# Offset convolution of a deformable layer: six products for four output rows in place of four products for two

## The chip, the cores and the metric

The kernel runs on one core of a Trainium2 chip. The time is the device time of one execution in microseconds (us); three executions of the kernel before gave 1509.89, 1511.71 and 1513.13 us, median 1511.71. A core has four compute engines that matter here, each with its own queue of instructions that it takes strictly in order: TensorE (PE, matrix products; its weight loads are listed apart as PEld), VectorE (DVE), ScalarE (ACT) and GpSimd (POOL). SyncE (SP) mostly starts DMA transfers. Products land in PSUM, eight banks of 2 KB per partition (512 f32 numbers each); DVE or ACT has to read them out from there before the bank is free again.

## The reference

`x` has 8 images of 128 channels, 64x64 pixels, float32. Two layers are applied, each as `x + layer(groupnorm(x))`:

```python
om  = conv3x3(x, off_w) + off_b              # 128 -> 27 channels
off, mask = om[:, :18], sigmoid(om[:, 18:])  # two offsets and a mask for each of 9 taps
val = bilinear_sample(x, tap position + off) * mask
y   = einsum('bckhw,ock->bohw', val, w) + b  # deformable 3x3 convolution, 128 -> 128
layer0 = relu(batchnorm(y) * gamma + beta)
layer1 = mixture of 4 expert 3x3 convolutions (top 2, gated per image) + shared 3x3 convolution
```

The change is in the first line, the 3x3 convolution to the 27 offset and mask channels, and only for images 1 to 7.

## The kernel before

**Stages.** `dense()` does layer 0 for all images, `layer1()` does layer 1. `general()` is a fallback for large offsets; it is compiled, and does not run with these inputs. All instructions of `dense()` are in the order in which the program writes them (a manual schedule): every engine's queue is the order of emission.

**Bands.** `dense()` walks over 64 bands `g`, eight for each image (`NB = 8`), each of eight output rows. For a band, `sample` (L704) multiplies transposed pixels `xts` by weights `s` in five groups `q`; the products `pq` (three PSUM buffers, L714) are copied by ACT into `samples` (L724). `weights` (L683, DVE, L698) makes `s` three groups ahead (`AHEAD = 3`): at the start of band `g` DVE first makes groups 3 and 4 of that band, then, after `put_off()` (statistics of the last output and `close`, which copies the edges of `samples`, L740 to L747), groups 0 to 2 of the next band. Then `conv(g - 1)` (L751) does nine products `py` (L763) for the band before, 18 after the last band of an image, as that one has two output spans.

**What runs between the taps.** After each tap of `conv` the loop at L867 emits a little of other work, by the number of the tap, "part": at 0, 1, 5, 6 a quarter of the next band's pixels is transposed (`pixels`, L665: PE product `pt` into PSUM tag `pc`, then an ACT copy); at 1, 3, 5, 7 half of the x weights is prepared (`spread`, L642: ACT L648, then DVE L650); at 4 `pick` (L652) copies the pixels of a later band on DVE. And it calls `tick()` three times for a tap (four in image 0; three for two taps where there are 18).

**The generator `tables(b)`.** Each `tick()` advances `tables(b)` by one `yield`. It makes everything that image `b` needs ahead of its own bands: group norm (L309 to L337, ACT and DVE normalise four chunks each), the offset convolution (L340 to L416), a turned copy of the result (L422), stores to DRAM (SP, L427, L432), loads in another layout (`raw_off`, L465, L452), then distances, masks and the tables for x and y (L505 to L582). `pause(n)` spends `n` ticks. `yield BLOCK` makes the generator wait until the next tap among 2, 3, 4, 7; that is for PSUM: the tag `pc` has one buffer, shared by the pixels and by the products of the offset convolution. For image `b + 2` the generator is started in band 7 of image `b` and is drained ahead of band 6 of image `b + 1`; for image 1 the first part is done ahead of band 0, and the rest runs in bands 1 to 5 of image 0.

**The offset convolution before.** It is a minimal-filtering scheme in the row direction: two output rows from four products instead of six. For each `j` in 1, 2, 0, 3 `combine(j)` (L348) makes a difference or a sum of two sets of rows of the normalised image in `combos[0]` or `combos[1]` (two DVE instructions of 128x1024), and `block(j)` (L392) does one product: three taps `kx`, each as four matmuls of 512 columns (504 at the edge taps), with 32 output channels each and the four quarters of the image side by side in PSUM (`pc[32 * q : 32 * q + 32]`). The combined weights `offu_sb` are made once at the start (L802 to L806). ACT and DVE gather the four products into `om` (L402, L408, L409, L413, L415). The block of `j = 1` falls into the first band of the image before (part 7), those of 2, 0, 3 into the second band (parts 2, 4, 7), for images 3 to 7; for image 1 into bands 1 and 2 of image 0 (part 7, then 2, 4, 7), for image 2 into bands 0 and 1 of image 1 (parts 3, 7, then 2, 3).

Of the kernel before, what the change touches and what calls it, by code (L numbers as in the profile page):

```python
# [8 lines left out]
F32 = mybir.dt.float32  # L9
I32 = mybir.dt.int32  # L10
AF = mybir.ActivationFunctionType
ALU = mybir.AluOpType
# [4 lines left out]
P = 128  # L17
H = W = 64
# [4 lines left out]
CH = 512  # L23
# [6 lines left out]
NE = 4  # L30
# [21 lines left out]
ROWPAD = REACH  # L52
# [4 lines left out]
BLOCK = "block"  # L57
# [7 lines left out]
def deform_moe_conv(  # L65
# [18 lines left out]
    nc = tc.nc  # L84
# [3 lines left out]
    small = ctx.enter_context(tc.tile_pool(name="small", bufs=2))  # L88
# [6 lines left out]
        out=gsel, in_=gsel, compare_op=ALU.is_ge, fill=0.0, base=0,  # L95
# [3 lines left out]
        out=gsel, in_=gsel, compare_op=ALU.is_ge, fill=0.0, base=3,  # L99
# [78 lines left out]
    def dense():  # L178

        with ExitStack() as st:  # L180
            st.enter_context(tc.manual_schedule())
            a1 = st.enter_context(tc.tile_pool(name="d1", bufs=1))
# [3 lines left out]
            ps_c = st.enter_context(tc.tile_pool(name="ps_c", bufs=1, space=PSUM))  # L186
# [9 lines left out]
            offw_sb = a1.tile([P, TAPS, 32], F32, name="offw_sb")  # L196
            nc.gpsimd.memset(offw_sb[:, :, 27:32], 0.0)

            offu_sb = [a1.tile([P, 3, 32], F32, name=f"offu_sb{i}") for i in range(2)]
            offb_sb = a1.tile([P, 1], F32, name="offb_sb")  # L200
            nc.gpsimd.memset(offb_sb, 0.0)
            ident = a1.tile([P, P], F32, name="ident")
# [60 lines left out]
            def pause(n):  # L263
                for _ in range(n):
                    yield
# [34 lines left out]
            def tables(b):  # L300
# [3 lines left out]
                pad = pads[b % 2]  # L304
# [43 lines left out]
                def combine(j):  # L348

                    lo, hi, op = (  # L350
                        (0, 2, ALU.subtract), (1, 2, ALU.add), (2, 1, ALU.subtract),
                        (1, 3, ALU.subtract),
                    )[j]
                    for half in range(2):
                        rows = [
                            pad[:, ROWPAD - 1 + H // 2 * half + i :][:, 0 : H // 2 : 2]
                            for i in (lo, hi)
                        ]
                        n = H // 4
                        (nc.vector if b or j == 1 or half == 0 else nc.gpsimd).tensor_tensor(  # L360
                            combo_of[j][:, half * n : half * n + n], *rows, op
                        )
                        yield from pause(2)
# [25 lines left out]
                def taken(j):  # L389
                    return pcs.pop(j).rearrange("p (t w) -> p t w", w=W)  # L390

                def block(j):  # L392

                    yield BLOCK
                    for kx in (1, 0, 2):
                        tap(j, kx)
                    yield from pause(2)

                for j in (1, 2):
                    yield from combine(j)  # L400
                yield from block(1)
                nc.scalar.activation(even, taken(1), AF.Identity, bias=offb_sb)  # L402
                yield from combine(0)
                yield from block(2)
                if b == 0:
                    yield from combine(3)
                m2 = taken(2)
                nc.vector.tensor_tensor(odd, even, m2, ALU.subtract)  # L408
                nc.vector.tensor_tensor(even, even, m2, ALU.add)  # L409
                if b:  # L410
                    yield from combine(3)
                yield from block(0)
                nc.vector.tensor_tensor(even, even, taken(0), ALU.add)  # L413
                yield from block(3)
                nc.vector.tensor_tensor(odd, odd, taken(3), ALU.subtract)  # L415
                yield  # L416
                by_rows = omr.rearrange("p (h w) -> p h w", w=W)
                turned = omc.rearrange("p w h -> p h w")
                for half in (slice(0, H // 8), slice(H // 8, H // 4)):
# [46 lines left out]
                        by_column.append((k, outs, parts, v))  # L466
                for k, *where in by_column:
                    turned_in(nc.sync if b or k == 0 else nc.gpsimd, k, *where)
                yield from pause(50)

                def moved(side, t, *dims):

# [373 lines left out]
            for g in range(len(bands) + 1):  # L846
                b, j = bands[g] if g < len(bands) else (B, 0)
                if j == NB - 2:
                    for _ in made:
                        pass  # L850
                    asked, made, means_of = True, iter(()), statistics(b + 2)
                turned = pixels(g + 1) if g + 1 < len(bands) else iter(())
                for q in range(NGR):
                    if g < len(bands):
                        if g or q + AHEAD < NGR:
                            weights(g * NGR + q + AHEAD)
                        sample(g * NGR + q)
                        if q == 2:
                            load_x(g + 3, nc.gpsimd)
                        if q in (2, 3):  # L860
                            for k in range(T * (q - 2), T * (q - 1)):
                                load_y(g + 2, k, nc.gpsimd)
                    if q == 1:
                        put_off()
                taps = conv(g - 1) if g else iter(())
                twice = 2 if g and bands[g - 1][1] == NB - 1 else 1
                for done, _ in enumerate(taps):  # L867
                    part, odd = divmod(done, twice)
                    if odd == 0 and part in PIXELS:
# [12 lines left out]
                    for _ in range(3 + (g < NB) if twice == 1 else 1 + done % 2):  # L882
                        tick()
                    if odd == 0 and part == 4:
                        if g + 2 < len(bands):
                            pick(g + 2)
                        if 2 <= j < 6:
                            load_quarter(b + 2, j - 2)
                for _ in turned:
                    pass  # L890
                if g == 0:
                    pick(2)
                    for slots in HALVES:
# [238 lines left out]


    def layer1():
        yscale = small.tile([P, 1], F32, name="yscale")
        rsqrt(yscale, ymv[:, 1:2], BN_EPS)
        nc.vector.tensor_tensor(yscale, yscale, gamma_sb, ALU.mult)
        yshift = small.tile([P, 1], F32, name="yshift")
        nc.vector.tensor_tensor(yshift, ymv[:, 0:1], yscale, ALU.mult)
        nc.vector.tensor_tensor(yshift, beta_sb, yshift, ALU.subtract)  # L1140
        with ExitStack() as st:
# [58 lines left out]
            def prepare(b, made):  # L1200
# [79 lines left out]
                tot = small.tile([P, 1], F32, name="tot")  # L1280
# [3 lines left out]
                mb = small.tile([P, NE], F32, name="mb")  # L1284
# [186 lines left out]
```

## Time and profile before

| what | us |
|---|---|
| median of three runs | 1511.71 (1509.89 to 1513.13) |
| profiled execution | 1505.04, of which the span of the profile is 1502.9 |
| PE, DVE, ACT, POOL busy | 1361.4, 973.0, 826.5, 503.8 |
| idle time of PE between 200 and 1010 us of the span | 28 of 810 |
| a group of the offset convolution on PE (24 records) | 2.76 |
| one `combine` instruction, 128x1024 (L360) | 1.22 |
| one addition from PSUM into `om`, 128x512 (L408) | 0.69 |

All lines in fences are from the profile of one execution. Times are us from the start of its span. A line of the order of time has the start, the duration from the first start to the last end, the engine, the line of the kernel, the operation, output and inputs by the program's names, the shape, and the number of instructions; in square brackets stands how long the engine was idle before it and what ended that. A float32 matmul is two records of PE, so a block of 12 matmuls is "x24". The windows view gives, for each stretch, the busy time of the engines in the order PE, PEld, DVE, ACT, POOL with the number of instructions in parentheses, then the granted PE clock (1.00 is full speed), and the DMA share and rate.

### The profile page before, as it was taken

The numbers are of one execution on the slowest core, as the hardware profiler recorded it, in microseconds if no ns is written. First come the engines' busy times: TensorE is split into PE (matmuls) and PEld (weight loads), VectorE is DVE, ScalarE is ACT, GpSimd is POOL, SyncE is SP. The second block draws the span as 40 slices with busy tenths as digits, with TensorE's granted clock in tenths as the row PEclk, the third lists the DMA queues.
The fourth block names the chain that finished last, engine by engine and source line by source line (L and its number), as shares of the span: only waits on it lengthen the run. The fifth ranks groups of instructions, "written<-read, shape, count | busy, mean of one in ns | idle before, by whom it ended". The sixth has DMA issues, their size and how long they took to land.

```text
span 1502.9 us, 21333 instructions
## 1 busy us (share of the span) xinstructions
PE 1361.4 (91%) x7714; PEld 761.9 (51%) x7714; DVE 973.0 (65%) x1904; ACT 826.5 (55%) x1123; POOL 503.8 (34%) x775
## 2 busy tenths in 40 slices
PE   4279799999999998999999999999974899999998
PEld 1245465656556555555555565566642344444443
DVE  5555475576567647656765765645518888889872
ACT  2365674776587468658757865866724233322320
POOL 6333342433334233333423433344203222333200
PEclk9589899999999999999999999999996999999999
DMA  4485775986698497669748876788607134444111
GB/s 145 115 172 132 170 163 109 210 189 137 129 210 190 96 199 196 136 130 206 191 100 192 211 150 132 164 200 190 148 23 303 56 141 168 168 167 154 56 43 58
DMA packets 130940, 227.28 MB, mean 151 GB/s; under 512 B 82003, under 2 KB 88303, under 8 KB 122137
## 3 DMA queue, kind: packets, MB, share of 16 engines
q0 software_dynamic: 50928, 122.40, 38.7%
q1 hardware_dynamic: 78880, 102.93, 22.1%
q8 instruction: 63, 1.03, 0.3%
q10 hardware_dynamic: 1017, 0.50, 0.1%
q14 instruction: 52, 0.43, 0.1%
HBM read 180.23 MB, written 45.35 MB: 150 GB/s over the span
## 4 chain that ended last, share of the span: by engine, by line
PE 67%; DMA 11%; ACT 10%; DVE 5%; issue 3%; SPq 3%; POOL 1%; ACTq 0%; DVEq 0%; POOLq 0%
PE py L763 22%; PE pc L1383 21%; PE pq L714 12%; PE pt L672 5%; PE pc L379 5%; DMA ywts<-taby 3%; DMA xwts<-tabx 2%; ACT xwts L648 2%; ACT xt L677 2%; ACT work L537 1%; ACT samples L724 1%; DMA pad<-in_x_dram 1%; ACT work L541 1%; SPq L432 1%; DMA colwise<-om 1%
## 5 line engine op out<-in xcount | busy, mean ns | idle before, releaser
L763 PE MATMUL py<-samples,dw_sb 128*128 128x512 f32 (+3 forms) x1296 | 576.9, 562 | 7.1 <-ACT y L771 5.3
L617 POOL DMA_DIRECT2D ywts<-taby x504 | 303.3, 618 | 281.4 <-DMA xwts<-tabx 236.0
L714 PE MATMUL pq<-s,xt 64*128 64x144 f32 (+1 forms) x3840 | 284.3, 301 | 34.3 <-DVE s L698 21.8
L724 ACT COPY samples<-pq 128x864 f32<-128x864 f32 (+1 forms) x320 | 280.7, 973 | 36.0 <-PE pq L714 35.8
L714 PEld LDWEIGHTS pq<-s,xt 64*128 64x128 f32 x3840 | 257.9, 190 | 83.1 <-issue 23.5
L763 PEld LDWEIGHTS py<-samples,dw_sb 128*128 128x128 f32 x1296 | 217.0, 190 | 160.3 <-issue 133.5
L677 ACT COPY xt<-pt 128x512 f32<-128x512 f32 (+1 forms) x256 | 142.2, 555 | 206.7 <-PE pt L672 206.3
L698 DVE TENSOR_TENSOR s<-xwts,ywts 128x72 f32<-128x72 f32 (+1 forms) x447 | 199.3, 499 | 84.1 <-PE pq L714 42.0
L650 DVE TENSOR_SCALAR xwts<-xwts 128x1152 f32<-128x1152 f32 (+2 forms) x130 | 97.4, 749 | 185.9 <-ACT xwts L648 185.7
L672 PEld LDWEIGHTS pt<-ident,picked 128*128 128x128 f32 x960 | 111.1, 141 | 170.5 <-ACT xt L677 103.9
L632 POOL DMA_DIRECT2D xwts<-tabx x128 | 73.0, 574 | 349.1 <-DVE s L698 307.6
L1383 PE MATMUL pc<-v,u 128*128 128x512 f32 x384 | 172.8, 599 | 9.6 <-DVE u L1331 9.6
L672 PE MATMUL pt<-ident,picked 128*128 128x128 f32 x960 | 153.1, 280 | 28.6 <-ACT xt L677 26.0
L1383 PE MATMUL pc<-v,wmix 128*128 128x512 f32 x384 | 176.4, 604 | 0.0
L648 ACT ACTIVATE xwts<-xwts,place 128x1152 f32<-128x1152 f32 (+2 forms) x130 | 161.0, 1242 | 11.6 <-DMA xwts<-tabx 11.6
L1361 ACT ACTIVATE t<-pc,bmix 128x512 f32<-128x512 f32 x32 | 22.0, 687 | 183.6 <-PE pc L1383 101.6
L1383 PEld LDWEIGHTS pc<-v,u 128*128 128x128 f32 x384 | 72.5, 190 | 98.6 <-issue 85.1
L1383 PEld LDWEIGHTS pc<-v,wmix 128*128 128x128 f32 x384 | 72.5, 192 | 89.1 <-issue 85.4
L360 DVE TENSOR_TENSOR combo<-pad 128x1024 f32<-128x1024 f32 x61 | 73.7, 1236 | 21.5 <-PE pc L379 14.4
L657 DVE COPY picked<-pad 128x960 f32<-128x960 f32 x128 | 82.0, 682 | 0.0
L771 ACT ACTIVATE y<-py,db_sb 128x512 f32<-128x512 f32 (+3 forms) x72 | 45.7, 635 | 65.6 <-PE py L763 31.0
L1210 POOL TENSOR_TENSOR x<-x,xt 128x512 f32<-128x512 f32 x32 | 45.4, 1452 | 86.1 <-ACT x L1208 86.1
(172 smaller groups left out, 1031.2 us busy)
## 6 DMA issues: line engine op xcount, KB each, us to landing
xwts<-tabx POOLq DMA_DIRECT2D x128, 576.0 KB, 7.7
ywts<-taby POOLq DMA_DIRECT2D x504, 90.0 KB, 8.2
pad<-in_x_dram SPq DMA_DIRECT2D x48, 512.0 KB
out_dram<-yo SPq DMA_DIRECT2D x32, 512.0 KB
yd<-y SPq DMA_DIRECT2D x48, 256.0 KB
pad<-yd SPq DMA_DIRECT2D x16, 512.0 KB
x<-yd SPq DMA_DIRECT2D x16, 512.0 KB
xt<-in_x_dram SPq DMA_DIRECT2D x16, 512.0 KB
```

What stands on the lines that cost most here:

```text
L379: nc.tensor.matmul(pcs[j][32 * q : 32 * q + 32].rearrange("p (h w) -> p h w", w=W)[:, :, lo:hi], lhsT=weight_of[j][:, kx], rhs=combo_of[j] ...
L617: engine.dma_start(out=y_wts[g % 2][at : at + NR * Q, r].rearrange("p a b c -> p (a b c)"), in_=bass.AP(tensor=y_table[b].tensor, offset=y ...
L648: nc.scalar.activation(part, part, AF.Abs, bias=column)
L650: nc.vector.tensor_scalar(part, part, -1.0, 0.0, ALU.add, ALU.min)
L657: nc.vector.tensor_copy(picked[g % 2][:, :, h], bass.AP(tensor=one.tensor, offset=one.offset, ap=[list(one.ap[0]), [T, NCOL], [W, Q], [1, Q]],
L672: nc.tensor.transpose(pt[:, c], picked[g % 2][:, c0 + c].rearrange("p h y x -> p (h y x)"), ident,)
L677: nc.scalar.copy(xts[g][:, c0 : c0 + n], pt[:, 0:n])
L698: engine.tensor_tensor(s[:, :, 3 * at : 3 * (at + k)].rearrange("p m (c x) -> p m c x", x=3), by_x[:, :, c : c + k], by_y[:, :, w : w + k] ...
L714: nc.tensor.matmul(by_m[:, h, :, at : at + k], lhsT=xts[g][rows, c], rhs=s[rows, :, at : at + k], start=True, stop=True,)
L724: nc.scalar.copy(bass.AP(tensor=one.tensor, offset=one.offset + first, ap=[list(one.ap[0]), [M * PLANE, 2], [PLANE, M], [WB + 1, 3], [1, w ...
L763: nc.tensor.matmul(py, lhsT=dw_sb[:, 3 * (2 - yy) + 2 - xx], rhs=samples[g % 2][:, m : m + 3 * n - 2 : 3, xx, 1 : W + 1], start=(i == 0), ...
L1383: nc.tensor.matmul(pc, lhsT=us[j][:, kx], rhs=vs[g][:, rows, kx : kx + W], start=(kx == 0), stop=(kx == 2),)
```

## The change

For images 1 to 7 the offset convolution uses the next larger scheme: four output rows from six products instead of twelve (the scheme before uses eight for four rows). Six weight sets are made from the three rows of the filter by `quad_weights()`, once, at the end of band 0: six DVE instructions and four ACT scalings of 128x96, into `offu_sb`, the new `offv_sb`, and over the middle row of `offw_sb`. `combine_pair(n)` makes two of the six row combinations at a time, each of 16 rows (128x1024), in the two halves of one `combos` buffer, by four DVE instructions; there are three pairs. `pair(n)` is one block: two products side by side in one PSUM bank, each of three taps by four matmuls of 256 columns. `om` is then gathered from quarters of 128x256: two by ACT, ten instructions on DVE. Image 0 keeps the old way. A pause ahead of the table part is 59 instead of 50 ticks for images 2 to 7. Counted tick by tick, the three blocks of images 3 to 7 fall into the first band at part 7 and the second at parts 2 and 4; those of image 1 into band 2 of image 0 at parts 2, 4, 7; those of image 2 into band 0 of image 1 at part 4 and band 1 at parts 2 and 4. From `distances_y` on, every step of `tables` is emitted at the same tap as before. Four small tiles of layer 1 have one buffer instead of two.

```diff
             offu_sb = [a1.tile([P, 3, 32], F32, name=f"offu_sb{i}") for i in range(2)]
+            offv_sb = a1.tile([P, 3, 32], F32, name="offv_sb")
+
+            quad_of = (
+                offw_sb[:, 0:3], offu_sb[0], offu_sb[1], offw_sb[:, 3:6], offv_sb, offw_sb[:, 6:9]
+            )
...
-                for j in (1, 2):
-                    yield from combine(j)
-                yield from block(1)
-                nc.scalar.activation(even, taken(1), AF.Identity, bias=offb_sb)
-                yield from combine(0)
-                yield from block(2)
+                quad = omr.rearrange("p (t i w) -> p i t w", i=4, w=W)
+                halves = [(t[:, 0 : H // 4], t[:, H // 4 :]) for t in combos]
+
+                def row(k):
+                    return pad[:, ROWPAD - 1 + k :][:, 0 : H - 3 : 4]
+
+                def mix(out, a, times, c):
+
+                    if times in (1, -1):
+                        op = ALU.add if times == 1 else ALU.subtract
+                        nc.vector.tensor_tensor(out, c, a, op)
+                    else:
+                        nc.vector.scalar_tensor_tensor(out, a, float(times), c, ALU.mult, ALU.add)
+
+                def combine_pair(n):
+
+                    lo, hi = halves[n % 2]
+                    for args in (
+                        (
+                            (lo, row(2), -4, row(4)), (hi, row(1), -4, row(3)),
+                            (lo, hi, 1, lo), (hi, hi, -2, lo),
+                        ),
+                        (
+                            (lo, row(2), -1, row(4)), (hi, row(1), -1, row(3)),
+                            (lo, hi, 2, lo), (hi, hi, -4, lo),
+                        ),
+                        (
+                            (lo, row(2), -1.25, row(0)), (lo, row(4), 0.25, lo),
+                            (hi, row(3), -5, row(5)), (hi, row(1), 4, hi),
+                        ),
+                    )[n]:
+                        mix(*args)
+                        yield from pause((2, 1, 1 + (b > 1))[n])
+
+                def pair(n):
+
+                    yield BLOCK
+                    pc = ps_c.tile([P, CH], F32, name="pc", tag="pc")
+                    for i, j in enumerate(((1, 2), (3, 4), (0, 5))[n]):
+                        weight = quad_of[j]
+                        for kx in (1, 0, 2):
+                            lo, hi = max(0, 1 - kx), min(W, W + 1 - kx)
+                            for q in range(4):
+                                nc.tensor.matmul(
+                                    pc[32 * q : 32 * q + 32, CH // 2 * i : CH // 2 * (i + 1)]
+                                    .rearrange("p (h w) -> p h w", w=W)[:, :, lo:hi],
+                                    lhsT=weight[:, kx],
+                                    rhs=halves[n % 2][i][
+                                        :, 4 * q : 4 * q + 4, lo + kx - 1 : hi + kx - 1
+                                    ],
+                                    start=(kx == 1), stop=(kx == 2),
+                                    skip_group_check=True,
+                                )
+                    pcs[n] = pc.rearrange("p (i t w) -> p i t w", i=2, w=W)
+                    yield from pause(2)
+
                 if b == 0:
...
+                else:
+                    yield from combine_pair(0)
+                    yield from combine_pair(1)
+                    yield from pair(0)
+                    first, second = pcs[0][:, 0], pcs[0][:, 1]
+                    nc.scalar.activation(quad[:, 0], first, AF.Identity, bias=offb_sb)
+                    yield
+                    nc.vector.tensor_tensor(quad[:, 1], quad[:, 0], second, ALU.subtract)
+                    nc.vector.tensor_tensor(quad[:, 0], quad[:, 0], second, ALU.add)
+                    yield from combine_pair(2)
+                    yield from pair(1)
+                    first, second = pcs[1][:, 0], pcs[1][:, 1]
+                    nc.scalar.copy(quad[:, 3], first)
+                    yield from pause(2)
+                    nc.vector.tensor_tensor(quad[:, 2], quad[:, 3], second, ALU.add)
+                    nc.vector.tensor_tensor(quad[:, 3], quad[:, 3], second, ALU.subtract)
+                    yield from pair(2)
+                    first, second = pcs[2][:, 0], pcs[2][:, 1]
+                    for at, a, times, c in (
+                        (0, 2, 1, 0), (2, 2, 3, 0), (1, 3, 2, 1), (3, 3, 6, 1),
+                    ):
+                        mix(quad[:, at], quad[:, a], times, quad[:, c])
+                    nc.vector.tensor_tensor(quad[:, 0], quad[:, 0], first, ALU.add)
+                    nc.vector.tensor_tensor(quad[:, 3], quad[:, 3], second, ALU.add)
+                    yield
...
-                yield from pause(50)
+                yield from pause(50 if b < 2 else 59)
...
+            def quad_weights():
+
+                v0, v1, v2, v3, v4, v5 = quad_of
+                nc.vector.tensor_tensor(v2, v0, v5, ALU.add)
+                nc.vector.tensor_tensor(v1, v2, v3, ALU.add)
+                nc.vector.tensor_tensor(v2, v2, v3, ALU.subtract)
+                nc.vector.scalar_tensor_tensor(v4, v5, 4.0, v0, ALU.mult, ALU.add)
+                nc.vector.scalar_tensor_tensor(v3, v3, 2.0, v4, ALU.mult, ALU.add)
+                nc.vector.scalar_tensor_tensor(v4, v4, 2.0, v3, ALU.mult, ALU.subtract)
+                for v, n in ((v1, -6.0), (v2, -6.0), (v3, 24.0), (v4, 24.0)):
+                    nc.scalar.activation(v, v, AF.Copy, scale=1.0 / n)
...
                     for slots in HALVES:
                         spread(2, slots)
+                    quad_weights()
...
-        yscale = small.tile([P, 1], F32, name="yscale")
+        yscale = small.tile([P, 1], F32, name="yscale", bufs=1)
```

More of the change, by code (lines that the diff above doesn't have):

```diff
@@ L397, in block @@
                     yield from pause(2)
-                for j in (1, 2):
-                    yield from combine(j)
-                yield from block(1)
-                nc.scalar.activation(even, taken(1), AF.Identity, bias=offb_sb)
-                yield from combine(0)
-                yield from block(2)
-                if b == 0:
-                    yield from combine(3)
-                m2 = taken(2)
-                nc.vector.tensor_tensor(odd, even, m2, ALU.subtract)
-                nc.vector.tensor_tensor(even, even, m2, ALU.add)
@@ L410, in tables @@
[L410 to L416, printed above, removed]
+                quad = omr.rearrange("p (t i w) -> p i t w", i=4, w=W)
+                halves = [(t[:, 0 : H // 4], t[:, H // 4 :]) for t in combos]
+                def row(k):
+                    return pad[:, ROWPAD - 1 + k :][:, 0 : H - 3 : 4]
@@ new lines, in tables @@
+                if b == 0:
+                    for j in (1, 2):
+                        yield from combine(j)
+                    yield from block(1)
+                    nc.scalar.activation(even, taken(1), AF.Identity, bias=offb_sb)
+                    yield from combine(0)
+                    yield from block(2)
+                    yield from combine(3)
+                    m2 = taken(2)
+                    nc.vector.tensor_tensor(odd, even, m2, ALU.subtract)
+                    nc.vector.tensor_tensor(even, even, m2, ALU.add)
+                    yield from block(0)
+                    nc.vector.tensor_tensor(even, even, taken(0), ALU.add)
+                    yield from block(3)
+                    nc.vector.tensor_tensor(odd, odd, taken(3), ALU.subtract)
+                    yield
[23 more added lines that the diff above has]
+                    nc.vector.tensor_tensor(quad[:, 3], quad[:, 3], second, ALU.add)
+                    yield
@@ L1134, in layer1 @@
     def layer1():
-        yscale = small.tile([P, 1], F32, name="yscale")
+        yscale = small.tile([P, 1], F32, name="yscale", bufs=1)
         rsqrt(yscale, ymv[:, 1:2], BN_EPS)
         nc.vector.tensor_tensor(yscale, yscale, gamma_sb, ALU.mult)
-        yshift = small.tile([P, 1], F32, name="yshift")
+        yshift = small.tile([P, 1], F32, name="yshift", bufs=1)
         nc.vector.tensor_tensor(yshift, ymv[:, 0:1], yscale, ALU.mult)
@@ L1279, in prepare @@
                 )
-                tot = small.tile([P, 1], F32, name="tot")
+                tot = small.tile([P, 1], F32, name="tot", bufs=1)
                 nc.vector.tensor_reduce(tot, wd, AX.X, ALU.add)
@@ L1283, in prepare @@
                 nc.vector.tensor_scalar(wd, wd, tot, None, ALU.mult)
-                mb = small.tile([P, NE], F32, name="mb")
+                mb = small.tile([P, NE], F32, name="mb", bufs=1)
                 nc.vector.tensor_tensor(mb, eb_sb, wd, ALU.mult)
```

## The prediction

> **What bounds the kernel now.** First the shares of the page, then the windows view.
>
> ```profile
> PE 1361.4 (91%) x7714; PEld 761.9 (51%) x7714; DVE 973.0 (65%) x1904; ACT 826.5 (55%) x1123; POOL 503.8 (34%) x775
> ```
>
> ```profile
> 360.00:490.00 130.00, 125.57 (x863) 74.67 (x863) 84.00 (x169) 88.65 (x118) 48.33 (x82) 1.00 0.75 167
> ```
>
> A whole image of 130 us leaves PE 4.4 us idle, at full clock, and DVE 46. So PE time taken out of `dense` counts, and DVE time added is free until it makes PE wait. DVE is strictly in order: what matters is where its new work stands. So next the order of time around the convolution for image 4 (images 3 to 7 look alike), DVE, then PE:
>
> ```profile
> 485.88 1.23 DVE L360 TENSOR_TENSOR combo<-pad 128x1024 f32<-128x1024 f32 x1 [0.78 <-ACT pad L332]
> 488.48 2.35 DVE L360 TENSOR_TENSOR combo<-pad 128x1024 f32<-128x1024 f32 x2
> 496.52 2.36 DVE L360 TENSOR_TENSOR combo<-pad 128x1024 f32<-128x1024 f32 x2 [2.42 <-PE pc L379]
> 498.79 1.27 DVE L698 TENSOR_TENSOR s<-xwts,ywts 128x432 f32<-128x432 f32 x3
> 508.44 0.69 DVE L408 TENSOR_TENSOR om<-om,pc 128x512 f32<-128x512 f32 x1 [4.91 <-PE pc L379]
> ```
>
> ```profile
> 493.73 2.76 PE L379 MATMUL pc<-combo,offu_sb 128*32 128x512 f32 x24
> 496.41 1.58 PE L763 MATMUL py<-samples,dw_sb 128*128 128x256 f32 x6
> 497.93 4.20 PE L714 MATMUL pq<-s,xt 64*128 64x216 f32 x60
> 516.47 2.76 PE L379 MATMUL pc<-combo,offw_sb 128*32 128x512 f32 x24 [0.21 <-ACT xt L677]
> ```
>
> See that the sample weights (498.79) follow the last combines directly, and that PE samples from 497.93: it needs group 3 after groups 0 to 2, about 500.4 (4.20 less some 1.7 for groups 3 and 4). DVE has it at 499.4. That is 1 us of slack.
>
> **PE: what a block costs.** The block at 493.73 holds PE until 496.41: 2.68 us, six sets of four matmuls side by side at 0.427 us each (512 columns, two records). A new block is twelve sets of 256 columns: if a set takes half as long, with 5 ns more for each, 2.74. Three for four saves 2.68 - 3 x 0.06 = 2.5 us an image, 17.5 for seven. No row shows sets this short. The upper bound is the sampling line: 60 matmul records in 4.20 us are 70 ns each, a set of four 0.28, a block 3.4. I take 2.74: sampling columns alone explain its rate (13 pairs-of-two at 0.24 and two at 0.36 are 3.8 us), so it shows no issue limit, and inside a block the loads hide:
>
> ```profile
> 493.76:493.80 0.04, 0.04 (x4) 0.04 (x8) 1.00 0.00 0
> 493.90:494.10 0.20, 0.20 (x4) 0.00 (x0) 1.00 0.00 0
> ```
>
> (Windows of L379 alone, PE then PEld: eight loads are running 0.07 us into the block beside the first four products, and none later.) A rule speaks against the change here: the Trainium skill, "TensorE: Matmul & The Clock Gate", "Measured speedup vs the span model", says that weight loads overlap running matmuls only when the row group differs, and these column tiles share all rows. By the rule each short set would pay its 0.11 us load and a block would be 4.0 us (estimate), and PE's own work would grow by 1.3 us an image, 9 for seven, where the row gives 17.5 less. The row contradicts the rule, and the sum goes by the row.
>
> **DVE: what is added.** Combines: 12 of 128x1024 where there were 8. Two take 2.35, so the next starts after 1.15; a dependent one after about 1.25 (L409 follows L408 by 0.72, the next work by 0.62). The fused form is priced like the plain one (0.751 at L549 against 0.749 at L574, both 64x576). So 14.4 for 9.2. Gathering: ten of 256 elements at 0.35 for four of 512 at 0.62 (0.69 each). Together +6 us an image, 43 in all, 6 of 46 idle.
>
> **Images 3 to 7, on DVE's queue in image 4's clock.** The first mix reads every fourth row of the whole image, so it starts when ACT's normalising ends, 485.88. Two mixes to 488.18, x weights (L650) to 488.86, two mixes to 491.3, pick 492.45, four mixes of pair 1 (not needed for block 0, but ahead in the queue) 497.25, L650 497.93, two gathers 498.65, two mixes of pair 2 501.05, sample weights 501.65, where they were ready at 499.4. Block 0 gets its pair at 491.3, in time for 493.73. PE waits from 500.4 to 501.65: 1.25. `close`, behind the weights, ends about 0.25 after PE wants to start the convolution. Then PE block 1 at about 507, block 2 at 511.5; the DVE reads of block 2 end at 515, when PE wants the buffer `pc` for pixels. At 516.47 no fourth block: 2.68 and its wait of 0.21 gone. Sum 1.25 + 0.25 + 0.2 (longer blocks) - 2.89 = -1.2 an image, -6.0 for five. ACT: two 256-column reads of about 0.47 (L771's 256 form) for one of 0.69, and both turned copies now ahead of the output's copy at 520: this uses up the gain there, without a stall by my count.
>
> **Image 4 once more.** The turned copies and stores are emitted three taps earlier, on SP ahead of the output store of that band (which nobody waits for soon: two `y` buffers). `raw_off` then lands some 5 us earlier. Second line:
>
> ```profile
> 170.82 3.46 PE L714 MATMUL pq<-s,xt 64*128 64x144 f32 x24 [7.03 <-DVE s L698]
> 568.36 1.86 PE L714 MATMUL pq<-s,xt 64*128 64x144 f32 x24 [3.54 <-DVE s L698]
> ```
>
> DVE had stood 2.05 and 2.17 waiting for `raw_off` (L503), so the 3.54 goes: -3.5 (bounds 0 and -3.5).
>
> **Start and image 1.** The parts of the start:
>
> ```profile
> 90.77 2.60 ACT L724 COPY samples<-pq 128x1008 f32<-128x1008 f32 x3
> 91.57 1.27 DVE L698 TENSOR_TENSOR s<-xwts,ywts 128x432 f32<-128x432 f32 x3
> 92.32 3.45 PE L714 MATMUL pq<-s,xt 64*128 64x144 f32 x24 [2.48 <-DVE s L698]
> 100.23 2.92 ACT L332 ACTIVATE pad<-pad,shift,scale 128x512 f32<-128x512 f32 x4
> 102.34 2.35 DVE L360 TENSOR_TENSOR combo<-pad 128x1024 f32<-128x1024 f32 x2
> 111.75 1.87 PE L714 MATMUL pq<-s,xt 64*128 64x144 f32 x24 [0.31 <-DVE s L698]
> ```
>
> `quad_weights` starts on DVE at 91.57, six dependent small ones at about 0.28 (L1331, 128x128: 0.29): 1.7; ACT's four scalings (0.28 at L806) end near 93.6, and the three copies behind them, which free PSUM for PE's fourth group, move by 2.8: PE starts at 94.6 instead of 92.32. Everything ACT does after PE follows, +2.3, so normalising ends at 105.45, where the first mix may start. Eight mixes, a pick and L650 later it is 116.8, first sample weights 117.45: PE at 117.5 instead of 111.75, +5.75, though it lost a block ahead of that. In band 2 the DVE chain gather, mix, mix, L650, mix, mix, gather after block 0 holds `pc` until 2.1 us after PE wants it. And after 6 us of idleness PE may be slow: the line at 170.82 took 3.46 where 1.9 is usual, that at 568.36 did not (bounds 0 and 1.5; 6 us is nearer to 7.03: 1.5). Sum +9.4. The later wait of 7.03 hangs on this image's own stores and moves along.
>
> **Image 2.** Block 0 comes one tap later, and its `pc` is held until 237.05 by the queue mix, mix, pick, gather: PE wants it at 234.35. 2.7 lost, 2.7 saved by the missing block at 237.51, 0.67 (the wait for ACT's `y` there) gained, about as much lost on ACT's turned copies: 0.
>
> **Priced at nothing.** POOL: x and y loads wait for DVE's sample weights (L698), 2.3 later; the last y load of that band is issued at 509.02, lands about 9.0 later and is used at 523.28, slack 5; if that cover went, 1 to 3 us an image. The 59 ticks leave all later steps at their taps. One-buffer tiles in layer 1: DVE in order.
>
> **Sum.** +9.4 + 0 - 6.0 - 3.5 = -0.1 on the profiled 1505.04 (span 1502.9 and 2.1 around it); that run lies 6.7 below the median, so 1511.6. Each DVE spacing off by 0.1 moves images 3 to 7 by about 1 us each, image 1 by 1: own range 1504 to 1519.
>
> **The rivals.**
> 1. *The backlog misses PE* (faster). If DVE ran pairs 1 and 2 in its idle stretches (2.42, 4.91) without passing 500.4, and image 1 lost only the 2.3 of the start: -17.5 - 3.5 + 2.3 = -18.7, 1493. Half of that, 1502, if only image 1 is better than worked out. For it: 46 us of idle DVE an image. Against: the idle lies behind block reads, not ahead of the weights. 0.26.
> 2. *Short sets are bound by issue* (slower). A block at 3.4 is 0.66 more; three an image, of which the first is hidden by the wait for the weights: +1.3 x 6, +8: 1519.5; it decides from a set of 0.24. At 0.32 it would be +2.5 x 6 = +15. Against: the windows above. 0.13.
> 3. *The loads become late* (slower). Stores moved earlier meet the x and y loads; DVE has waited 28.5 us for `ywts` between 200 and 1100. One more wait of 2 us that reaches PE per image: +14, less if two: 1519 to 1526. 0.10.
> 4. *My sum*, 0.51: of that 0.20 below 1508.7, 0.19 within, 0.12 above.
>
> **How the numbers follow.** 0.2% is 3 us, about what three runs spread by. Faster 0.26 + 0.20 = 0.46; same 0.19; slower 0.13 + 0.10 + 0.12 = 0.35. The range leaves out the far half of rival 1 and the worst of 2 and 3: 1498 to 1522.
>
> **What would show it.** Right: L379 blocks of 2.8 us with records of about 0.37; PE in the second band waiting 1 to 1.5 us for DVE s; PE at the fourth group of band 2 six us late; no wait near 568. Wrong: blocks over 3 us; waits for DVE s under 0.5 (then rival 1); new waits for `ywts`.

## The result, and the profile after

The kernel after takes 1513.11 us (median of 22 executions, 1507.45 to 1517.59). Executions of the kernel before, run beside them, took 1517.94 (22 executions, 1505.64 to 1527.99). The ratio is 0.998, interval 0.9961 to 0.9999 (the two medians alone lie 4.8 us, or 0.3%, apart): slightly faster, and little more than nothing. The absolute time is within 1.5 us of the forecast of 1511.6, but that is luck: the forecast started from a time of the kernel before that was 6.2 us too low, and it forecast no change against it (-0.1), where there were -4.8.

The shares on the page of the kernel after, and one whole image in the windows view (PE, PEld, DVE, ACT, POOL, then the PE clock, the DMA share and rate):

```profile
PE 1353.5 (90%) x8050; PEld 782.8 (52%) x8050; DVE 1015.3 (67%) x1980; ACT 829.2 (55%) x1134; POOL 502.2 (33%) x775
```

```profile
360.00:490.00 130.00, 125.34 (x921) 78.23 (x920) 89.32 (x177) 89.84 (x120) 49.31 (x83) 1.00 0.76 169
```

DVE has 42 us more, 43 were worked out. PE has only 7.9 less, where three blocks for four should save 17.5: some 5 of the missing 9.6 are products at a lower clock in the start (below); the rest was not traced. Next the order of time of the kernel after around block 0 of image 4, on DVE, then on PE:

```profile
499.82 2.36 DVE L416 SCALAR_TENSOR_TENSOR combo<-pad 128x1024 f32<-128x1024 f32 x2 [1.94 <-ACT pad L337]
506.35 2.34 DVE L414 TENSOR_TENSOR combo<-pad 128x1024 f32<-128x1024 f32 x2
508.73 2.48 DVE L416 SCALAR_TENSOR_TENSOR combo<-combo 128x1024 f32<-128x1024 f32 x2
512.58 1.22 DVE L416 SCALAR_TENSOR_TENSOR combo<-pad 128x1024 f32<-128x1024 f32 x1
513.84 1.23 DVE L416 SCALAR_TENSOR_TENSOR combo<-pad,combo 128x1024 f32<-128x1024 f32 x1
514.98 1.26 DVE L784 TENSOR_TENSOR s<-xwts,ywts 128x432 f32<-128x432 f32 x3
```

```profile
507.63 2.77 PE L449 MATMUL pc<-combo,offu_sb 128*32 128x256 f32 x48
510.33 1.58 PE L849 MATMUL py<-samples,dw_sb 128*128 128x256 f32 x6
511.85 2.60 PE L800 MATMUL pq<-s,xt 64*128 64x216 f32 x36
515.73 1.86 PE L800 MATMUL pq<-s,xt 64*128 64x144 f32 x24 [1.28 <-ACT samples L810]
525.61 2.77 PE L449 MATMUL pc<-combo,offw_sb 128*32 128x256 f32 x48
```

A block with two products takes 2.70 us (507.63 to 510.33; 2.74 was worked out), and no fourth one follows. The sample weights stand behind the first two mixes of pair 2 on DVE (512.58, 513.84), start at 514.98, 15.2 us after the first mix (15.8 were worked out), and PE waits 1.28 for its fourth sample group, where 1.25 was forecast. The label names ACT's copies; run e6 shows that it is these weights.

The start is where the kernel after loses most. PE in its order of time, from band 1 to band 5 of image 0:

```profile
95.72 3.49 PE L800 MATMUL pq<-s,xt 64*128 64x144 f32 x24 [4.74 <-ACT samples L810]
99.14 1.86 PE L849 MATMUL py<-samples,dw_sb 128*128 128x448 f32 x2
119.94 3.49 PE L800 MATMUL pq<-s,xt 64*128 64x144 f32 x24 [6.96 <-DVE s L784]
138.82 0.68 PE L758 MATMUL pt<-ident,picked 128*128 128x128 f32 x4 [2.11 <-DVE om L493]
146.90 2.60 PE L800 MATMUL pq<-s,xt 64*128 64x216 f32 x36
185.51 3.49 PE L800 MATMUL pq<-s,xt 64*128 64x144 f32 x24 [7.08 <-DVE s L784]
```

The line at 146.90, the start of band 3's samples, stood at 132.26 before: 14.6 us lost. The waits of 6.96 and 2.11 are the ones worked out (the line at 119.94 had waited 0.31 before; 2.1 was forecast for `om`); that of 7.08 is the 7.03 of before, moved along. What was not worked out is what follows each wait. The windows view after these waits, kernel before, then after (the last window of after stands behind the wait of 2.11, which before did not have):

```profile
95.70:99.00 3.30, 3.30 (x16) 1.94 (x15) 1.16 (x3) 2.03 (x3) 2.87 (x6) 1.00 0.61 161
111.70:113.60 1.90, 1.85 (x25) 1.60 (x25) 1.86 (x7) 1.77 (x3) 1.03 (x2) 1.00 0.71 220
113.60:118.00 4.40, 4.40 (x23) 2.13 (x26) 1.69 (x4) 3.18 (x5) 3.50 (x7) 1.00 0.91 223
```

```profile
99.10:103.00 3.90, 3.90 (x14) 2.23 (x13) 2.97 (x8) 1.62 (x2) 2.30 (x5) 0.66 0.97 232
119.90:123.40 3.50, 3.46 (x25) 2.98 (x25) 3.47 (x10) 0.91 (x1) 2.65 (x5) 0.50 0.46 102
123.30:128.00 4.70, 4.70 (x16) 2.25 (x14) 0.17 (x1) 2.17 (x4) 2.56 (x5) 0.75 1.02 213
138.80:143.20 4.40, 4.38 (x15) 2.10 (x19) 2.93 (x6) 2.22 (x3) 0.00 (x0) 0.61 0.01 4
```

The same work ran at the full clock before, and runs at 0.50 to 0.75 after. Later PE makes good part of it: block 0 of images 3, 4, 5, 6 and 7 starts 15.5, 13.9, 9.6, 9.5 and 8.2 us later than in the profile of before (379.68 against 364.21 and so on), and the two spans, 1511.3 and 1502.9, differ by 8.4. So the two profiles say 8 us slower and the medians say 5 us faster. The profiled execution of after, 1513.05, is a typical one; that of before, 1505.04, was 12.9 below its median. That gap, as much as the change, is what the experiments had to explain.

### The profile page after: what moved, and what is told of

The parts are those of the page before. It is cut to its first block, busy times and chain, and to the rows that moved or that the text cites. A ratio compares the mean times of both kernels' runs of the same rounds, so it can differ in the third digit from the quotient of the medians.

```text
span 1511.3 us, 22074 instructions
## 1 busy us (share of the span) xinstructions
PE 1353.5 (90%) x8050; PEld 782.8 (52%) x8050; DVE 1015.3 (67%) x1980; ACT 829.2 (55%) x1134; POOL 502.2 (33%) x775
## 4 chain that ended last, share of the span: by engine, by line
PE 62%; DMA 13%; ACT 11%; DVE 7%; issue 4%; POOL 1%; SPq 1%; ACTq 0%; DVEq 0%; POOLq 0%
PE py L849 22%; PE pc L1482 21%; PE pq L800 10%; DMA xwts<-tabx 5%; PE pt L758 5%; DMA ywts<-taby 4%; PE pc L449 3%; ACT samples L810 2%; ACT xwts L734 2%; ACT xt L763 2%; ACT work L623 2%; DVE s L784 1%; ACT work L627 1%; DVE combo L416 1%; ACT pad L337 1%
## 5 line engine op out<-in xcount | busy, mean ns | idle before, releaser
L800 PE MATMUL pq<-s,xt 64*128 64x144 f32 (+1 forms) x3840 | 287.6, 302 | 44.8 <-DVE s L784 23.6
L1309 POOL TENSOR_TENSOR pad<-pad,pad 128x512 f32<-128x512 f32 x28 | 39.5, 1438 | 71.8 <-ACT pad L1307 71.7
```

The lines of the kernel that those rows point to most:

```text
L800: nc.tensor.matmul(by_m[:, h, :, at : at + k], lhsT=xts[g][rows, c], rhs=s[rows, :, at : at + k], start=True, stop=True,)
L1309: adder.tensor_tensor(y, y, xt[:, c * CH : (c + 1) * CH], ALU.add)
```

## The experiments

The theory: (a) the products of images 2 to 7 gain about what was worked out, less a stall of some 1.25 us an image behind the sample weights; (b) image 1 and the weight sets at the start lose more than that, because of the clock; (c) the earlier stores take away waits for `raw_off` that vary from one execution of before to the next. Rivals: the loss at the start is what all the images pay; the gain is from the products alone and the order of the stores does nothing; the kernel before is simply noisy.

All runs were compared with executions of the kernel before beside them on the same chip: e1 to e4 together (before 1518.70), e5 to e8 (1517.31), e9 to e12 (1516.73). Times are medians.

**e1 and e2: the two kernels again.** No edit.

> The kernel before, unchanged, for a second profile. In the first one it took 1505 us, 13 us under its median of 22 runs, and the changed kernel's profile (1511.3 span) is 8 us longer, while the runs say that it is 0.2% shorter. Theory A: the first profile caught an execution with fewer waits than usual; this profile is longer, 1510 to 1525, and has more idle time of PE in bands of images 2 to 7 (PE waiting for DVE s behind raw_off or y loads: over 10 us between 200 and 1104, where the first had 3.9). Theory B: what varies lies elsewhere, in the start (before 200 us) or in layer 1; then PE's waits between 200 and 1104 stay within 5 us of the first profile's 28.

> The changed kernel, unchanged, beside the kernel before. Ratio 0.996 to 1.000. Theory A: its bands of images 3 to 7 repeat the first profile within 2 us (128 to 129 us an image), as its stores are earlier. Theory B: it varies from profile to profile as much as the kernel before.

The kernel before against itself gives 1.0009 (0.9982 to 1.0036), the kernel after 0.9988 (0.9966 to 1.001), 1515.49 us. What e1 shows is in its trace: another execution of the same program, 1511.83 us, the shortest of its 12. Lines of PE's order of time in e1:

```profile
566.18 1.86 PE L714 MATMUL pq<-s,xt 64*128 64x144 f32 x24 [1.71 <-DVE s L698]
700.11 3.45 PE L714 MATMUL pq<-s,xt 64*128 64x144 f32 x24 [5.61 <-DVE s L698]
864.08 1.87 PE L714 MATMUL pq<-s,xt 64*128 64x144 f32 x24 [2.22 <-DVE s L698]
```

In the profile before there was one such wait, 3.54 at 568.36. Here there are three of over 1 us, and the longest, 5.61, costs a further 1.6 as its group takes 3.45 instead of 1.87. The first two stand behind DVE's waits for `raw_off` (2.14 ahead of 560.92 and 4.24 ahead of 693.93, both L503), in the tables of images 4 and 5. So this wait is no property of image 4: it falls on whichever images had their loads late. The third is of another kind: DVE had waited 5.87 for `ywts` ahead of 855.53, with no distances near it. The view of waits for PE from 200 to 1110 us (total, times, longest), before, e1, then e2:

```profile
PE pq L714 <- DVE s L698: 3.9, 2, 3.5
```

```profile
PE pq L714 <- DVE s L698: 9.9, 4, 5.6
```

```profile
PE pq L800 <- DVE s L784: 2.0, 1, 2.0
```

The kernel after is not steady either, and here the expectation for e2 was missed. From block 0 of image 3 to that of image 4 PE takes 127.95 us in the profile after, 131.44 in e2 and 133.37 in e12; the stretches of the later images agree within 1.5 us. In e2 and e12 DVE waits 2.97 and 3.38 for `ywts` ahead of the last group norm statistics of the next image, PE then waits 1.83 and 2.25 for these (`mv`, L302), and slower products follow: in e12 PE's granted clock is 0.51 from 487 to 494 us.

**e3: image 1 with the old products.** Image 1 keeps four products for two rows, the weight sets are made three bands later, images 2 to 7 stay as after.

```diff
-                if b == 0:
+                if b < 2:
                     for j in (1, 2):
                         yield from combine(j)
...
-                    yield from combine(3)
+                    if b == 0:
+                        yield from combine(3)
                     m2 = taken(2)
...
+                    if b:
+                        yield from combine(3)
...
                         spread(2, slots)
+                if g == 3:
                     quad_weights()
```

> Images 0 and 1 the old way, images 2 to 7 the new way; the weight sets are made at the end of band 3 instead of band 0. My reading of the two traces: the start and image 1 cost the changed kernel 14 us (PE reaches band 3 of image 0 at 146.9 instead of 132.3). If that is a real loss, this kernel is 12 to 15 us faster than the changed one, ratio to before 0.988 to 0.991. Rival: PE's delay there is made up later, as the loads for image 1's bands (7 us of waiting at 170 to 185 in both traces) set the pace; then the gain is under 4 us.

Measured: 0.9891 (0.986 to 0.9922), 1501.76 us, 13.7 less than e2 beside it. PE samples of band 3 start at 133.28, after the 132.26 of before. So the start and image 1 cost 13.7 (9.4 had been forecast), and what is left, images 2 to 7 with the earlier stores, is worth -16.9, where -9.5 had been forecast. Both halves of the sum were too small, and that they nearly cancel is luck.

**e4: the stores where they were.** Images 2 to 7 have their stores and the loads behind them at the old ticks; the turned copies stay early (24.0 us after block 0 in image 4, as in the kernel after; 26.3 in the kernel before), and the products are as after.

```diff
-                yield from pause(4)
+                yield from pause(4 if b < 2 else 13)
                 for j in range(4):
...
-                yield from pause(50 if b < 2 else 59)
+                yield from pause(50)
```

> The changed kernel with the stores of the offsets (and the raw_off loads behind them) of images 2 to 7 emitted at the taps of the kernel before, three taps later (13 ticks ahead of the stores, 50 behind, instead of 4 and 59). If the earlier stores take waits for raw_off and the y loads out of the bands behind, this kernel is 4 to 12 us slower than the changed one, with PE waiting 2 to 4 us for DVE s in some images. Rival: nothing hangs on the stores; within 2 us of the changed kernel.

Measured: 1.0 (0.997 to 1.0029), 1519.26 us, 3.8 more than e2, with intervals that overlap. But its trace, of an execution of 1529.47 us, the second longest of 12, has the waits back that e2 has not, 10.0 us between 200 and 1110 us, four times. The longest on PE, and DVE's order of time ahead of it:

```profile
716.52 3.49 PE L800 MATMUL pq<-s,xt 64*128 64x144 f32 x24 [5.55 <-DVE s L784]
```

```profile
708.28 0.32 DVE L589 TENSOR_SCALAR combo<-combo,nudge 128x192 f32<-128x192 f32 x1 [2.36 <-DMA combo<-colwise]
711.83 0.32 DVE L589 TENSOR_SCALAR combo<-combo,nudge 128x192 f32<-128x192 f32 x1 [3.23 <-DMA pad<-in_x_dram]
715.77 1.25 DVE L784 TENSOR_TENSOR s<-xwts,ywts 128x432 f32<-128x432 f32 x3
```

DVE stands at the first step of the distances, 2.36 and 3.23 for loads (the label of the second names one of `x`), and the sample weights in its queue behind them are late. Not all four waits are of this kind: one of 1.96 at 351.67 follows a wait of DVE for `ywts`. In the kernel after no wait of DVE at these lines for a DMA is listed between 200 and 1100 us, nor in e2.

**e5: the weight sets ahead of band 0.** They are made before the first sample weights, instead of in band 0.

```diff
+            quad_weights()
             AHEAD = 3
...
                         spread(2, slots)
-                    quad_weights()
```

> The changed kernel with the six weight sets made ahead of band 0, where DVE waits 1.8 us and ACT 6.4 us anyway, instead of at the end of band 0. If the weights' ten small instructions delay PE's fourth group of band 1 (95.7 instead of 92.3) and ACT's normalising behind it (104.9 instead of 100.2), this takes out 3 to 5 us. Rival: image 1 is bound by DVE's eight mixes alone, which the weights do not touch; then under 1.5 us.

Measured: 0.9958 (0.9931 to 0.9986), 1510.07 us, 3 to 5 below the kernel after (1513.11, and 1513.39 and 1515.49 in its repeats, in other groups of runs), as was expected. Two lines of PE's order of time in e5:

```profile
93.31 1.87 PE L800 MATMUL pq<-s,xt 64*128 64x144 f32 x24 [1.44 <-DVE s L784]
116.56 3.49 PE L800 MATMUL pq<-s,xt 64*128 64x144 f32 x24 [5.47 <-DVE s L784]
```

The first is PE's fourth group of band 1, 2.4 us earlier than after and at its full rate (1.87 against 3.49), and the second the fourth group of band 2, 3.4 earlier; band 3 starts 3.6 earlier, at 143.29. So the weight sets are some 3.5 of the 14, and the rest is the mixes of image 1 ahead of its sample weights, as the prediction placed it.

**e6: pair 2 behind the sample weights.** For images 3 to 7 all four mixes of pair 2 are emitted after the weights.

```diff
-                        yield from pause((2, 1, 1 + (b > 1))[n])
+                        yield from pause((2, 1, 1 + (b == 2))[n])
...
+                    yield from pause(4 if b > 2 else 0)
                     yield from combine_pair(2)
```

> The changed kernel with the four mixes of the third pair, for images 3 to 7, emitted in the first taps of the second band, behind its sample weights, where now two of them stand ahead (four ticks of pause ahead of the pair, one tick for each mix). The sample weights should then be ready some 2.4 us earlier and PE's wait ahead of its fourth group there (1.25 to 1.28 in each of these images) should go; no other block moves. 4 to 6 us less than the changed kernel. Rival: the wait belongs to ACT, as the profile's label has it (samples copies); then it stays at 1.2 and the time within 2 us.

Measured: 0.994 (0.9916 to 0.9963), 1507.69 us, some 6 less than after (5.4 to 7.8, by which group the kernel after is taken from). The lines of image 4 in the order of time of e6, DVE, then PE:

```profile
509.31 1.26 DVE L785 TENSOR_TENSOR s<-xwts,ywts 128x432 f32<-128x432 f32 x3
513.95 1.22 DVE L416 SCALAR_TENSOR_TENSOR combo<-pad 128x1024 f32<-128x1024 f32 x1
```

```profile
504.36 2.77 PE L449 MATMUL pc<-combo,offu_sb 128*32 128x256 f32 x48
508.57 4.20 PE L801 MATMUL pq<-s,xt 64*128 64x216 f32 x60
```

All 60 sampling records run in one stretch of 4.20, with no wait ahead of the fourth group. The stall was DVE's queue, whatever the label said.

**e7 and e10: e3 and e6 together**, the same kernel in two groups of runs, no further edit.

> Images 0 and 1 the old way, with the weight sets at the end of band 3, and the late mixes for images 3 to 7. If both losses are real and add up: 1495 to 1499, ratio to before 0.984 to 0.988. If the late mixes only move the wait, 1502 as with the old image 1 alone.

> The same kernel as e7_both (old image 1, weight sets at the end of band 3, late mixes), beside the old convolution with early loads, for the difference of these two on one chip: 6 to 10 us less than that one if the products themselves pay, within 3 us if the transfers were all of it.

Measured: 0.9889 (0.9862 to 0.9916) and 0.9861 (0.9835 to 0.9886), 1498.10 and 1496.02 us: the fastest version here, faster than both kernels by about 1%. Both times lie in the 1495 to 1499 that was expected if the two gains add up; by the ratios that is less sure, as e7's 0.9889 is hardly below e3's 0.9891, and only e10's 0.9861 is.

**e8 and e11: the kernel before with its transfers earlier.** Old products everywhere. For images 2 to 7 the stores are emitted one tap earlier and the `raw_off` loads three taps earlier; one reduction on DVE (`most`) moves by a tap with them.

```diff
-                yield from pause(4)
+                yield from pause(4 if b < 2 else 1)
...
-                yield from pause(16)
+                yield from pause(16 if b < 2 else 10)
...
-                yield from pause(50)
+                yield from pause(50 if b < 2 else 59)
```

> The kernel before, its convolution untouched, with the stores of the offsets of images 2 to 7 one tap earlier and the raw_off loads behind them three taps earlier, at the tap of the changed kernel (pauses 1, 10, 59 instead of 4, 16, 50). If the time of these transfers is what costs the kernel before its waits of 1.7 to 5.6 us for DVE s around the distances, it is 4 to 9 us faster than before and these waits are gone from its profile. Rival: the gain of the changed kernel comes from its products alone; then within 2 us of before.

> The same kernel as e8_before_early: the convolution before with early raw_off loads. Ratio 0.992 to 0.996, and less than the changed kernel by 3 to 7 us.

Measured: 0.9941 (0.9915 to 0.9968) and 0.9961 (0.9933 to 0.9988): 9.3 and 7.6 us gained, no product changed. On one chip, e11 took 1509.09 us and the kernel after (e12) 1513.39. The executions also lie closer together, 1504.72 to 1510.90 in 7 of e8 and 1505.91 to 1516.87 in 9 of e11, against 1505.21 to 1525.07 in 18 and 1506.90 to 1525.81 in 20 of before beside them. So the time of these transfers does something by itself.

What moves is the loads. SP issues the turned stores 33.9 us after block 0 in all four traces, before, e1, e8 and e11, as they wait there for the second turned copy (in image 4 of the profile before it ends at 527.64, and the stores are issued from 527.66); it has issued the last `raw_off` load 58.1 to 61.4 us after block 0 in before and e1, 52.5 to 58.8 in e8 and e11, and 46.7 to 48.4 in the kernel after (images 3 to 7). DVE's waits for these loads at the distances add up to 4.7 us in the profile before and 8.2 in e1; in e8 and e11 none is listed. PE's waits for DVE s do not all go with them, e8, then e11:

```profile
PE pq L714 <- DVE s L698: 2.9, 3, 1.7
```

```profile
PE pq L714 <- DVE s L698: 6.5, 4, 2.7
```

The longest of these (2.69 at 861.15 in e11) stands behind a wait of DVE for `ywts` of 6.41. How the gain of 7.6 to 9.3 us is made up is therefore not shown: the two profiled executions of before, 1505.04 and 1511.83 us, are both well under the medians.

e10 beside e11 has the new products and the late mixes, with the loads emitted at the same taps, and is 13.1 us faster, more than the 6 to 10 that were expected: the new products pay for images 2 to 7, once nothing waits for them. Part of this can still be transfers, as e10 has issued its last `raw_off` load 45.1 to 46.4 us after block 0.

**e9: image 1 old, stores and loads late.** The edits of e3 and e4 together.

> Images 0 and 1 the old way, images 2 to 7 the new way, but stores and raw_off loads three taps later, as in the kernel before: the new products alone, with neither the loss of image 1 nor the gain of the earlier transfers. By my working 1.2 us for each of images 3 to 7 and nothing for image 2: 4 to 8 us under before, ratio 0.995 to 0.9975. Rival: without the earlier transfers the new products bring nothing, ratio 0.999 or more.

Measured: 0.9917 (0.9895 to 0.994), 1503.07 us: 13.7 us gained, more than was expected, and only a little less than e3, whose interval overlaps. Its trace has waits for DVE s of 1.59, 2.94 and 2.24, but none of 5 us as e1 and e4 have. So the two gains, earlier transfers with the old products (8.5, from e8 and e11) and new products with late transfers (13.7), don't add up to what both together bring (16.9): once the new products are there, the earlier transfers are worth some 3 to 4 (e9 against e3, e4 against e2, with intervals that overlap). A reason can be seen in the traces: as three blocks end sooner than four, the turned copies are earlier, and SP issues the turned stores 30.0 us after block 0 in e9 and e4, where the kernel before has 33.9. So the new products take away part of the same lateness; how much of the 13.7 that is was not measured. Why the long waits come back in e4, which differs from e9 only in image 1 and the start, no run here tells.

**e12: the kernel after again.** No edit.

> The changed kernel once more, on the chip of these three. Ratio 0.996 to 0.999.

Measured: 0.9982 (0.9962 to 1.0002), 1513.39 us, as the result.

## Why the prediction was wrong, point by point

- *What a block costs: right.* 2.70 to the next product, 2.77 long, 2.74 forecast. Rival 2 falls, and with it the rule of the Trainium skill ("TensorE: Matmul & The Clock Gate", section "The mechanism", just ahead of the section that the prediction names) that was weighed against the change: by it a block would have been 4.0 us (estimate). One reading was wrong without harm: weight loads do run later in the block before than 0.07 us, 24 in all with 0.68 us of busy time, beside products that are busy 2.68 of 2.71.
- *DVE, +6 us an image: right*, 42 us in all against 43.
- *Images 3 to 7, -1.2 each: right in the mechanism, the size open.* The stall was 1.28 against 1.25, it was where it was put, and e6 shows that it is the backlog. From block 0 of one image to that of the next, the kernel after takes 1.6, 0.8, 0.1 and 1.4 us less than before (with the 3.54 taken out), 0.9 on average. That is one execution against one, and the first of these stretches was 3.5 and 5.4 us longer in e2 and e12. In the medians the new products of images 2 to 7 are worth 13.7 with late transfers (e9), where -6.0 was forecast, and about 8 with early ones (16.9 less 8.5).
- *Image 2, 0:* the stall of 2.7 was measured as 2.99 at 251.54, and the image lost under 1 us.
- *Start and image 1, +9.4: too small, 14.6 in the trace and 13.7 by e3.* The waits were right. The failed term is the clock, put at 1.5 for one place. By the lines: 1.1 us more at the start before any of this, as ACT had its x tables later (89.56 against 88.46); 1.3 us of slow products behind the 4.74, which delay ACT's normalising and so all that follows; 2.7 instead of 1.5 behind the 6.96, as the clock is still 0.75 after the group; 1.5 behind the 2.11, which had been given no clock term. 9.4 + 1.1 + 1.3 + 1.2 + 1.5 is 14.5.
- *Image 4 once more, -3.5 with the bounds 0 and -3.5: the step that failed.* The mechanism was right: earlier loads, no wait at the distances. But the wait was read as one of image 4 in the single execution that was profiled, where it is a wait that comes in several images and changes from execution to execution. With the old products e8 and e11 give the earlier transfers 9.3 and 7.6 us, more than twice the bound; how large the gain can be could not be read from one trace. As e9 shows that this gain and that of the products overlap, only their sum is firm: -6.0 and -3.5 were forecast for images 2 to 7, and e3 measures -16.9. How it divides between the two terms depends on which is put in first.
- *The base: the profiled execution was taken to lie 6.7 below the median.* Against 22 executions it lay 12.9 below. The three times shown, 1509.89 to 1513.13, are among the five shortest of the 22.
- *Rival 1* falls: the backlog did reach PE, 1.28 in image 4 and 6.96 behind the mixes of image 1. That e3's 1501.76, by the old products in image 1, lies at its 1502 is coincidence, as the base had moved by 6.2. *Rival 3*: DVE did wait longer for `ywts` (40.1 us between 200 and 1110, 28.5 before). PE hardly felt it in the profile after; in e2 and e12 it did, with the waits for `mv` of 1.83 and 2.25.

## What to carry to other kernels

Ask of a wait for a DMA in one trace whether it is a property of that place or a sample of something that varies: a second profile, and times of more than three executions, tell; a change that happens to move the transfer may be worth more than its arithmetic. A step that changes two things is best judged in halves; here the half that helped (later images) and the half that hurt (the first image, where DVE had no room ahead of the sample weights) were each about three to five times the net (13.7 and 16.9 against 3.2 to 4.8). And work added to an in-order engine costs by where it stands: the same two mixes an image behind the sample weights instead of ahead of them were worth some 6 us in e6.

## What the runs showed of the hardware that was not expected

A wait of PE can cost more than its length. After waits of 4.7 to 7 us the sampling group of 24 records took 3.49 instead of 1.86 in the kernel after, at a granted clock of 0.50, and the following 4 us ran at 0.66 to 0.82: about 2.7 us on top of the 6.96. In the kernel before, the wait of 7.03 at 170.82 was followed by 0.51 too, but after 3.4 us by 1.00. A wait of 2.11 at 138.82 was followed by 0.61 over 4.4 us, and the one of 2.25 in e12 by 0.51 over 7 us, with a stretch from image 3 to image 4 that was 5.4 us longer than in the profile after; one of 3.54 in the profile before was followed by 1.00:

```profile
568.30:570.30 2.00, 1.95 (x25) 1.71 (x26) 1.97 (x7) 2.00 (x3) 0.96 (x2) 1.00 0.56 167
```

What tells these apart is not shown by these runs. And the kernel before spreads over 22 us between executions, 1505.64 to 1527.99. The two profiles of it that were taken, 1502.9 and 1509.7 us of span, differ by 6.8, and PE's waits for DVE s by 6.0 of that; for the longer executions no run shows where the time goes.
